# A three-stage spectral layer and a temporal layer on one core: the order of one hand-written period list

## The chip, the cores and the metric

The kernel runs on one core of one Trainium2 chip. The metric is the device time of one execution in microseconds (us). Three executions of the kernel before took 4318.21, 4323.12 and 4324.39 us; the median is 4323.12 us. Names of engines are those of the profile: PE (matmuls), PEld (loads of a matmul's weights), DVE, ACT, POOL (three engines for elementwise work), SP (a queue that only issues DMAs).

## The reference, cut to what matters

The input `x` is (4, 256, 256, 64) in float32: four images of 256 x 256 points with 64 channels. Two layers follow each other.

```python
h  = layernorm(x) @ w_te + b_te                        # 64 -> 128
F  = fft2(h)                                           # over both image axes
fc = gelu(concat(real(F), imag(F)) @ w_fc + b_fc)      # 256 -> 256, at every frequency
sp = real(ifft2(re(fc) + 1j * im(fc)))
x1 = x + sp @ w_tp + b_tp
d  = gelu(depthwise_conv3x3(layernorm(x1) @ w_fe + b_fe))
x2 = x1 + d @ w_fp + b_fp                              # end of layer 0
...
trend = moving_average(x2, 25)                         # layer 1, along the first image axis
out   = trend + irfft(W * rfft(x2 - trend)[:128])      # W mixes frequencies, per channel
```

## The kernel before, in words

**Three streams.** Layer 0 is cut into three pipelines that run beside each other.

- The *forward* stream takes columns of `x`, two at a time, 32 chunks for each image. It loads a chunk (`fl`), computes layernorm (the ops below that begin with f), folds it (`fa`, `fb`, `fh0`, `fh1`), transforms it along the height with matmuls (`y0`, `y1`), copies the result out of PSUM (`yt0`, `yt1`) and stores it to DRAM (`y_d`).
- The *spectral* stream takes pairs of frequencies from `y_d`: transform along the width (`x`, copied by `xs`), mix of channels for two halves (`m0`, `m1`; copied by `gc0`, `gc1`; added by `b0`, `b1`; GELU by `g0`, `g1`; folded by `p0`, `p1`), projection (`z`, copied by `zs`), a transpose (`w`, copied by `zt`), and the way back along the width (`u`, copied by `us`, combined by `uc`, `uf`, which also store to `u_d`).
- The *convolution* stream takes chunks of eight columns, 32 for each image: load from `u_d` (`ul`, `UL`) and from `x` (`xl`, `XL`), transform back along the height (`s`), residual (`r0`, `r1`), layernorm (the ops that begin with c), transposes (`t0`, `t1`, copied by `tt0`, `tt1`), sums for a fast convolution (`T0`, `T1`), products (`gm`, `gh`, `em`, `eh`), their evictions and sums (`gc_0`, `gc_1`, `ec0`, `ec1`, `cf0`, `cf1`, `sp0`, `sp1`), GELU (`a0`, `a1`), projection (`o0`, `o1`, copied by `fs0`, `fs1`), transposes back (`ft0`, `ft1`) and the residual with the store (`st0`, `st1`).

Layer 1 (`layer1`, L1494) follows when all of layer 0 is done.

**What sets the order.** A schedule of PE, DVE, ACT and POOL is recorded by hand: each of these engines runs its instructions in the order in which the Python code calls the ops, and waits on semaphores for the others. SP's queue is not in that schedule; its order is chosen by the tool that builds the program. The order of the ops is a list of words such as `g1:-3`, one list for each phase. `period(n)` (L1679) walks a list once: word `op:k` runs `op` for chunk `n + k` (for the ops of the spectral pairs, two of them for each n, for pair `2(n - 35) + k`). `do` (L1636) runs an op's predecessors first where they have not run yet (`FOLLOWS`, `EARLY`); what has run already is not run again. The list `FULL` (L1585) serves the periods n = 72 to 131, 60 of them, in which all three streams are alive. Lists `MIXED` and `CONV` serve the later periods.

**PSUM.** In this phase six PSUM banks are shared by all matmuls (`BANKS`, L27). `bank` (L158) hands out the bank that has been free longest, in the order of the recording; `free` (L182) returns a bank when its evicting op is recorded. So the order of the list also decides whose eviction a matmul waits for. If no bank is free, `make_room` (L168) pulls an eviction forward.

**Engines and lines of the ops that the prediction uses.** PE: `s` L1041, `t0` `t1` L1088, `w` L823, `z` L805, `m0` `m1` L750, `y0` `y1` L615, `x` L725, `u` L856, `gm` and `em` L1166, `gh` and `eh` L1180, `o0` `o1` L1283, `ft0` `ft1` L1308. ACT: `gc0` `gc1` L764, `g0` `g1` L775, `fq` and `cq` L279 (squares), `fR` and `cR` L288 and L289, `cA` L354, `cB` L364, `cC` L375, `cp` L395 and L396 (steps of the reciprocal root), `xs` L740, `zs` L813, `zt` L833, `us` L873, `yt0` `yt1` L633, `tt0` `tt1` L1098 to L1100, `gc_0` L1209, `gc_1` L1212, `ec0` `ec1` L1200, `a0` `a1` L1276, `fs0` `fs1` L1294. DVE: `b0` `b1` L770, `st0` `st1` L1322, `fm` `cm` L294, `fr` `cr` L283, `cM` L315 (seed of the root), `r0` L1054, `r1` L1062, `cf0` L1233 and L1234, `cf1` L1239 to L1245, `fa` L582, `fb` L602, `uc` L887 and L888, `uf` L907 and L920. POOL: `p0` `p1` L781, `fh0` `fh1` L609, `fx` and `cx` L410, `sp0` `sp1` L1218, `T0` `T1` L1124 to L1132, and the small products of the root, L355, L365, L376, L397.

**Buffers.** Most tiles of the spectral stream have two buffers; `zs`, `xb` (written by `fh0`, `fh1`), `yt`, `xn` (written by `cx`) and `sq` have one.

Of the kernel before, what the change touches and what calls it, by code (L numbers as in the profile page):

```python
# [136 lines left out]
def conv_seq_kernel(ctx: ExitStack, tc: tile.TileContext, a: dict, tables: bass.AP, out: bass.AP):  # L137
    nc = tc.nc
    x = a["x"]
# [11 lines left out]
        x="xs", m0="b0", m1="b1", z="zs", w="zt", u="uc", s="r1", t0="tt0", t1="tt1", gm="cf0",  # L151
        em="ec1", o0="fs0", o1="fs1", ft0="st0", ft1="st1", y0="yt0", y1="yt1",
# [1421 lines left out]
    def numbered(text):  # L1574

        return [(w.split(":")[0], int(w.split(":")[1]) if ":" in w else 0) for w in text.split()]

    follows = {}
    for line in FOLLOWS.replace("\n", "|").split("|"):
# [3 lines left out]


    FULL = numbered("""  # L1585
        g1:-3 uc:-3 em:-4 eh:-4 b0:-2 ec1:-4 cm:-1 gh:-4 m0:-1 gc_0:-4 ec0:-4 a0:-5 cf0:-4 p0:-3
        g0:-2 m1:-1 fr:-1 fh1:-3 p1:-3 z:-3 gc1:-1 gc0:-1 b1:-1 fq:-1 o0:-5 fs0:-5 o1:-5 cx:-2
        fs1:-5 fh0:-3 b0:-1 y0:-3 ft0:-5 g1:-2 sp0:-4 w:-4 st0:-5 zs:-3 p0:-2 fR:-1 fm:-1 cc:-1
        yt0:-3 ft1:-5 fC:-3 p1:-2 fp:-2 xl XL t1:-2 ul fM:-1 fA:-2 st1:-5 sp1:-4 tt1:-2 s cl t0:-2
        w:-3 gc_1:-4 tt0:-2 r0 r1 cM:-1 fx:-2 T0:-2 T1:-2 z:-2 m1 gc1 fB:-2 y1:-3 yt1:-3 uf:-3 zs:-2  # L1590
        cr UL:1 x:1 xs:1 g0:-1 u:-2 x:2 b1 us:-2 m0 zt:-4 xs:2 gc0 zt:-3 cf1:-4 fl a1:-4 cA:-1 Ta:-2
        cB:-1 cq gm:-3 fa:-2 fb:-2 cC:-1 cR cp:-1
    """)

    MIXED = numbered("""
# [204 lines left out]
```

## Time and profile before

| | value |
|---|---|
| median of three executions | 4323.12 us |
| profiled execution, its own time | 4325.4 us |
| its span, first to last instruction | 4323.6 us |
| PE busy over the span | 4158.0 us, 96% |
| DVE, POOL, ACT busy | 3453.4, 3163.4, 2961.5 us (80, 73, 68%) |
| mean granted clock of PE | 0.984 |
| one period of `FULL` in the steady part | 26.9 us |

The profiled execution is 1.8 us outside its span, and 2.3 us over the median. A line of the timeline has the start and the length in us, engine, source line, operation, the tile that it writes and those that it reads, the shape, how many instructions were merged into the line, and in brackets how long the engine stood idle before it and what ended that. Each matmul stands in the records twice. [...] What PE achieves is read from the distance between starts.

The times of `r0` (L1054), one for each convolution chunk, give the length of every period. In `FULL`, the periods from 984 to 1549 us, from 1580 to 1661 us and from 1869 to 2380 us are of 26.9 us with few exceptions. The first five periods, the change from the first to the second image (one gap of 68 us for two periods), the few periods behind it and the last three differ.

### The profile page before, as it was taken

How to read it: one execution, taken by the hardware profiler on the slowest of the kernel's cores; microseconds unless marked ns; L12 is line 12 of the kernel's file. 1: busy time of each engine (PE TensorE's matmuls, PEld its weight loads, DVE VectorE, ACT ScalarE, POOL GpSimd, SP SyncE). 2: the span in 40 equal slices, each digit the busy share in tenths (PEclk: the TensorE clock that was granted, in tenths of full speed). 3: DMA queues.
4: the chain of work that ended last, by engine and by line, in shares of the span. 5: the costliest groups of instructions: out<-in, count | busy, mean ns of one | idle time of the engine just before them, and what ended most of it. 6: DMA issues, size and time to landing. Idle time of an engine off the chain costs nothing.

```text
span 4323.6 us, 67389 instructions
## 1 busy us (share of the span) xinstructions
PE 4158.0 (96%) x22443; PEld 2315.2 (54%) x22443; DVE 3453.4 (80%) x5234; ACT 2961.5 (68%) x5409; POOL 3163.4 (73%) x3156
## 2 busy tenths in 40 slices
PE   8999999899999999899999999999998899999999
PEld 4544444345555555455555566666665566654444
DVE  6968999779999998899999878888887799962222
ACT  3338998678888887788888777888885466641111
POOL 6869999688888887788888877888887588840000
PEclk9999999989999999999999999999999999999999
DMA  6664555535454544444444443344433544439995
GB/s 190 211 190 142 161 161 162 152 98 137 137 137 137 137 137 124 122 122 138 138 138 129 113 109 109 106 112 112 118 98 91 173 113 118 114 108 358 342 343 228
DMA packets 763906, 655.28 MB, mean 152 GB/s; under 512 B 46413, under 2 KB 657695, under 8 KB 755240
## 3 DMA queue, kind: packets, MB, share of 16 engines
q1 hardware_dynamic: 726696, 583.84, 46.5%
q10 hardware_dynamic: 36864, 67.13, 4.1%
q8 instruction: 180, 2.95, 0.3%
q14 instruction: 166, 1.36, 0.1%
HBM read 364.81 MB, written 286.00 MB: 151 GB/s over the span
## 4 chain that ended last, share of the span: by engine, by line
PE 42%; POOL 6%; DVE 4%; DMA 4%; ACT 3%; issue 1%; SPq 1%; ACTq 0%; POOLq 0%; DVEq 0%
PE ps_o L1504 9%; PE ps_h_c L1166 5%; PE ps_p L750 3%; PE ps_s_c L1041 3%; PE ps_h_c L1180 3%; PE ps_f_c L1283 3%; PE ps_hh_c L1166 2%; PE ps_z L805 2%; PE ps_t_c L1088 2%; PE ps_u L856 2%; PE ps_x L725 2%; PE ps_ft_c L1308 2%; DMA out_dram<-oc 1%; PE ps_zt L823 1%; POOL xb L609 1%
## 5 line engine op out<-in xcount | busy, mean ns | idle before, releaser
L770 DVE TENSOR_TENSOR g<-ps_p,g 128x512 f32<-128x512 f32 x1040 | 702.2, 683 | 127.9 <-ACT g L764 109.7
L781 POOL TENSOR_TENSOR g<-g 128x512 f32<-128x512 f32 (+1 forms) x520 | 677.9, 1315 | 98.5 <-ACT g L775 88.8
L775 ACT ACTIVATE g<-g,b_fc 128x1024 f32<-128x1024 f32 (+1 forms) x520 | 598.3, 1151 | 1.5 <-DVE g L770 1.4
L750 PE MATMUL ps_p<-xs,wp 64*128 64x512 f32 (+1 forms) x2080 | 561.1, 615 | 9.9 <-DVE g L770 2.7
L1166 PE MATMUL ps_h_c<-td,wc_main 128*128 128x256 f32 x2048 | 517.1, 391 | 7.3 <-DVE s_c L1234 0.8
L764 ACT COPY g<-ps_p 128x512 f32<-128x512 f32 (+1 forms) x520 | 298.0, 585 | 268.5 <-PE ps_p L750 101.1
L1504 PE MATMUL ps_o<-xc,mt 128*128 128x512 f32 x1024 | 443.3, 595 | 3.9 <-DVE oc L1518 3.8
L1166 PEld LDWEIGHTS ps_h_c<-td,wc_main 128*128 128x128 f32 x2048 | 370.1, 193 | 122.5 <-ACT zt L833 36.7
L1276 ACT ACTIVATE h_c<-h_c,b_conv 128x1024 f32<-128x1024 f32 x256 | 297.6, 1164 | 140.6 <-DVE h_c L1245 54.1
L1518 DVE TENSOR_SCALAR oc<-ps_o,b_fp 128x512 f32<-128x512 f32 x128 | 93.5, 749 | 351.4 <-DMA out_dram<-oc 196.7
L1516 ACT ACTIVATE oc<-ps_o,b_fp 128x512 f32<-128x512 f32 x128 | 86.2, 686 | 363.0 <-PE ps_o L1504 196.7
L1128 POOL TENSOR_TENSOR td<-tt 128x512 f32<-128x512 f32 x256 | 327.0, 1299 | 10.0
L1504 PEld LDWEIGHTS ps_o<-xc,mt 128*128 128x128 f32 x1024 | 195.3, 191 | 251.2 <-issue 236.0
L609 POOL TENSOR_TENSOR xb<-xt 128x512 f32<-128x512 f32 x224 | 285.4, 1282 | 54.5 <-DVE xt L602 41.1
L750 PEld LDWEIGHTS ps_p<-xs,wp 64*128 64x128 f32 x2080 | 189.3, 186 | 239.6 <-issue 84.7
L805 PE MATMUL ps_z<-g,w_tp 128*64 128x512 f32 x1024 | 288.7, 617 | 24.6 <-POOL g L781 19.9
L725 PEld LDWEIGHTS ps_x<-tab,yb 128*64 128x64 f32 x4064 | 235.0, 138 | 133.3 <-issue 69.2
L1322 DVE TENSOR_TENSOR st<-x_c,ps_ft_c 128x256 f32<-128x256 f32 x512 | 261.8, 602 | 44.4 <-PE ps_ft_c L1308 41.4
L615 PE MATMUL ps_y<-xb,tab 128*64 128x512 f32 x1024 | 273.4, 623 | 23.3 <-POOL xb L609 17.1
L1283 PE MATMUL ps_f_c<-h_c,w_fp 128*64 128x512 f32 x1024 | 266.3, 615 | 15.6 <-ACT h_c L1276 15.5
L1180 PE MATMUL ps_h_c<-td,wc_half 64*128 64x256 f32 (+1 forms) x2048 | 278.6, 396 | 2.4 <-POOL td L1132 1.1
L1041 PE MATMUL ps_s_c<-uc_c,tab 64*128 64x512 f32 x1024 | 259.6, 616 | 15.6 <-DVE uc_c L990 8.7
(201 smaller groups left out, 9559.4 us busy)
## 6 DMA issues: line engine op xcount, KB each, us to landing
y_d<-yt SPq DMA_DIRECT2D x256, 256.0 KB, 3.6
yb<-y_d SPq DMA_DIRECT2D x256, 256.0 KB, 4.0
u_d<-ut SPq DMA_DIRECT2D x256, 256.0 KB, 3.6
x_c<-in_x_dram SPq DMA_DIRECT2D x512, 128.0 KB, 3.6
x_d<-st SPq DMA_DIRECT2D x128, 512.0 KB, 5.1
xc<-x_d SPq DMA_DIRECT2D x64, 1024.0 KB, 8.5
out_dram<-oc ACTq DMA_DIRECT2D x256, 256.0 KB, 5.8
xt<-in_x_dram SPq DMA_DIRECT2D x504, 128.0 KB, 2.5
```

The lines of the kernel that those rows point to most:

```text
L609: engine.tensor_tensor(sums[j][:, i], x0, x1, (ALU.add, ALU.subtract)[i])
L750: nc.tensor.matmul(ps[:, :nf], wp[rows, cols], rhs[rows], start=True, stop=r == 1 or not pr["special"],)
L770: nc.vector.tensor_tensor(gt[:, i], re, gt[:, 1], op)
L775: nc.scalar.activation(g, g, AF.Gelu, bias=b_fc[:, half : half + 1])
L781: nc.gpsimd.tensor_tensor(g[:, 0], g[:, 0], g[:, 1], op)
L805: nc.tensor.matmul(ps[r * C : (r + 1) * C, :nf], w_tp, d[:, :nf], start=True, stop=True)
L1041: nc.tensor.matmul(pss[i], tb[i * C : (i + 1) * C], uc[i * C : (i + 1) * C, ::-1, 1 - r, :] if down else uc[i * C : (i + 1) * C, :, r, :], ...
L1128: tt_(new[:, k : k + 3 : 2], a_c, nb_e, op)
L1166: nc.tensor.matmul(product(j, k, par), wc_main[:, par, k, :], td[:, k, slots(j)].rearrange("p j q -> p (j q)"), start=k in (0, 1, 3), stop ...
L1180: nc.tensor.matmul(product(j, k, par)[:, dst.start * Q : dst.stop * Q], wc_half[lo : lo + C, k, :], td[lo : lo + C, k, src].rearrange("p j ...
L1283: nc.tensor.matmul(ps[par * C : (par + 1) * C], w_fp, gs[j][:, :, par, i0 : i0 + 2, :].rearrange("p r j q -> p r (j q)"), start=True, stop ...
L1504: nc.tensor.matmul(ps[:, :nf], mts[i // CM][:, i % CM, t, to * P : (to + 1) * P], xc[:, t, :, :, i, :], start=t == 0, stop=t == 1,)
```

## The change

Only the list `FULL` changes; no instruction is added or removed in any stream.

```diff
     FULL = numbered("""
-        g1:-3 uc:-3 em:-4 eh:-4 b0:-2 ec1:-4 cm:-1 gh:-4 m0:-1 gc_0:-4 ec0:-4 a0:-5 cf0:-4 p0:-3
-        g0:-2 m1:-1 fr:-1 fh1:-3 p1:-3 z:-3 gc1:-1 gc0:-1 b1:-1 fq:-1 o0:-5 fs0:-5 o1:-5 cx:-2
-        fs1:-5 fh0:-3 b0:-1 y0:-3 ft0:-5 g1:-2 sp0:-4 w:-4 st0:-5 zs:-3 p0:-2 fR:-1 fm:-1 cc:-1
-        yt0:-3 ft1:-5 fC:-3 p1:-2 fp:-2 xl XL t1:-2 ul fM:-1 fA:-2 st1:-5 sp1:-4 tt1:-2 s cl t0:-2
-        w:-3 gc_1:-4 tt0:-2 r0 r1 cM:-1 fx:-2 T0:-2 T1:-2 z:-2 m1 gc1 fB:-2 y1:-3 yt1:-3 uf:-3 zs:-2
-        cr UL:1 x:1 xs:1 g0:-1 u:-2 x:2 b1 us:-2 m0 zt:-4 xs:2 gc0 zt:-3 cf1:-4 fl a1:-4 cA:-1 Ta:-2
-        cB:-1 cq gm:-3 fa:-2 fb:-2 cC:-1 cR cp:-1
+        g1:-3 em:-4 b0:-2 ec1:-4 cm:-1 gh:-4 m0:-1 ec0:-4 fh1:-3 gc_0:-4 cf0:-4 a0:-5 g0:-2 m1:-1
+        p0:-3 fq:-1 p1:-3 z:-3 gc1:-1 fr:-1 gc0:-1 fs0:-5 o0:-5 o1:-5 b1:-1 fa:-3 fs1:-5 fh0:-3
+        b0:-1 y0:-3 ft0:-5 g1:-2 fR:-1 sp0:-4 cx:-2 w:-4 ft1:-5 st0:-5 zs:-3 p0:-2 fC:-3 yt0:-3
+        cc:-1 xl fm:-1 p1:-2 t1:-2 ul tt1:-2 sp1:-4 fp:-2 fM:-1 s cl fl t0:-2 w:-3 fA:-2 st1:-5
+        gc_1:-4 fx:-2 r0 XL tt0:-2 r1 cM:-1 uf:-3 zs:-2 gc1 T0:-2 T1:-2 m1 UL:1 fB:-2 y1:-3 cA:-1 cr
+        g0:-1 yt1:-3 u:-2 x:2 b1 zt:-4 us:-2 zt:-3 m0 xs:2 cf1:-4 z:-2 x:1 xs:1 gc0 a1:-4 Ta:-2
+        cB:-1 fb:-2 cq gm:-3 cC:-1 uc:-2 cR cp:-1 eh:-3
     """)
```

With the pulls of `do` and `make_room` resolved, a steady period (the same in every one) reads on each engine as follows. Indices are those of the list; ACT is written from the same point, `g1:-3`. In `FULL`, `fA`, `fB`, `fC` and `fp` do nothing, since the root of the forward stream is taken together with that of the convolution stream in `cA` to `cp`.

```
PE   before  em eh gh m0:-1 m1:-1 z:-3 o0 o1 y0 ft0 w:-4 ft1 t1 s t0 w:-3 z:-2 m1:0 y1 x:1 u x:2 m0:0 gm
PE   after   the same circle, with u ahead of x:1
DVE  both    uc b0:-2 cm cf0 fr b1:-1 b0:-1 st0 fm st1 r0 r1 cM uf cr b1:0 cf1 fa fb
ACT  before  g1:-3 ec0 ec1 gc_0 a0 g0:-2 gc1:-1 gc0:-1 fq fs0 fs1 g1:-2 zs:-3 fR yt0 tt1 gc_1 tt0
             gc1:0 yt1 zs:-2 xs:1 g0:-1 us zt:-4 xs:2 gc0:0 zt:-3 a1 cA Ta cB cq cC cR cp
ACT  after   g1:-3 ec0 ec1 gc_0 a0 g0:-2 fq gc1:-1 gc0:-1 fs0 fs1 g1:-2 fR zs:-3 yt0 tt1 gc_1 tt0
             zs:-2 gc1:0 cA g0:-1 yt1 zt:-4 us zt:-3 xs:1 xs:2 gc0:0 a1 Ta cB cq cC cR cp
POOL before  p0:-3 fh1 p1:-3 cx fh0 sp0 p0:-2 p1:-2 sp1 fx T0 T1 cA cB cC cp
POOL after   fh1 p0:-3 p1:-3 fh0 sp0 cx p0:-2 p1:-2 sp1 fx T0 T1 cA cB cC cp
```

The calls that issue DMAs on SP stand in the order `xl XL ul st1 cl yt1 uf UL x fl` before and `xl ul cl fl st1 XL uf UL yt1 x` after. In the built programs the queue of a steady period is nearly the same in both: `xt` (four loads), the store of `st`, part of the four loads of `x_c`, two stores to `u_d`, two to `y_d`, two loads of `yb`, the rest of `x_c`, `uc`; one or two loads of `x_c` change places with these.

The last eviction that a matmul's PSUM bank waits for changes with the list (an op that takes two banks has two). `ft0` and `w:-4` also exchange theirs (`b1:-1` and `fs0`); ops not named keep theirs:

| matmul | before: banks freed by | after: banks freed by |
|---|---|---|
| `o1` | `gc1:-1` | `gc1:-1` |
| `s` | `st0`, `zs:-3` | `st0`, `zs:-3` |
| `w:-3` | `st1` | `tt1` |
| `z:-2` | `tt1` | `st1` |
| `m1:0` | `tt0`, `r0` | `r0`, `tt0` |
| `y1` | `r1` | `r1` |
| `u` | `yt1`, `zs:-2` | `zs:-2`, `gc1:0` |
| `x:1` | `gc1:0` | `yt1` |
| `x:2` | `xs:1` | `zt:-4` |
| `m0:0` | `b1:0`, `us` | `b1:0`, `us` |
| `gm` | `zt:-4`, `xs:2` | `zt:-3`, `xs:1` |
| `em` | `gc0:0`, `zt:-3` | `xs:2`, `gc0:0` |

(`em` is named here by the evictions of the period that it follows.)

## The prediction

> **What bounds the kernel now.** I read the page first, then the busy time by stretches, then the timeline of one steady period of `FULL` engine by engine, then the waits.
>
> ```profile
> span 4323.6 us, 67389 instructions
> PE 4158.0 (96%) x22443; PEld 2315.2 (54%) x22443; DVE 3453.4 (80%) x5234; ACT 2961.5 (68%) x5409; POOL 3163.4 (73%) x3156
> ```
>
> PE is busy 96% of the span. The list `FULL` rules 60 of the periods, some 1650 us. Two steady stretches of 18 periods each:
>
> ```profile
> 1065.00:1549.40 484.40, 480.48 (x2879) 265.76 (x2877) 451.47 (x670) 409.73 (x787) 426.64 (x397) 1.00 0.50 138
> 1868.90:2353.10 484.20, 480.77 (x2882) 265.55 (x2881) 451.64 (x667) 409.02 (x787) 427.28 (x397) 1.00 0.49 137
> ```
>
> Columns: stretch, length, busy time of PE, PEld, DVE, ACT, POOL, PE's clock, DMA share, GB/s. 484.4 / 18 = 26.9 us for a period. By busy time PE has no more than 0.2 us of it left, which would be 10 us in all. But a busy PE can hide a wait, so I compare starts of equal work:
>
> ```profile
> 1226.35 0.38 PE L1088 MATMUL ps_t_c<-ident,xn_c 128*128 128x128 f32 x2
> 1226.88 0.63 PE L823 MATMUL ps_zt<-ident,zs 128*128 128x128 f32 x4
> ...
> 1235.07 2.34 PE L1166 MATMUL ps_h_c<-td,wc_main 128*128 128x256 f32 x8
> 1237.25 1.89 PE L1166 MATMUL ps_hh_c<-td,wc_main 128*128 128x256 f32 x8
> 1238.98 1.89 PE L1166 MATMUL ps_h_c<-td,wc_main 128*128 128x256 f32 x8
> ```
>
> Eight records of the same shape take 2.18 us to the next line at 1235.07 (`gm`) and 1.73 at 1237.25. Record by record, starts are 0.216 apart when nothing is waited for; in `gm` three of the distances are 0.32, 0.46 and 0.32. The first 0.10 also stands in every change of row layout (1240.80, 1251.06) and stays; the other 0.35 is a wait. Likewise transposes follow each other in 0.109 us, but `w:-3` comes 0.386 after the last transpose of `t0` (1226.50 to 1226.88), and its second is 0.03 late: 0.30 of wait. Who ended them:
>
> ```profile
> 1226.13 0.61 DVE L1322 TENSOR_TENSOR st<-x_c,ps_ft_c 128x256 f32<-128x256 f32 x1
> ...
> 1249.85 1.08 DVE L1322 TENSOR_TENSOR st<-x_c,ps_ft_c 128x256 f32<-128x256 f32 x2
> 1251.39 1.25 DVE L294 TENSOR_REDUCE var_c<-sq 128x16 f32<-128x1056 f32 x1 [0.46 <-ACT sq L289]
> ```
>
> ```profile
> 1235.22 0.59 ACT L740 COPY xs<-ps_x 128x512 f32<-128x512 f32 x1 [0.88 <-PE ps_p L750]
> ```
>
> `st1` ends at 1226.74, 0.14 before `w:-3`, whose bank it frees. `xs:2` ends at 1235.81, 0.05 before the third record of `gm`, whose second bank it frees. `xs:2` itself starts only when `m0:0` has read the buffer that it overwrites, with ACT idle 0.88 us.
>
> [...]
>
> **The change part by part.** I walk one period, all times in the frame above (`z:-3` starts at 1245.31 before), lengths from the rows of the trace. From the end of an eviction to the matmul that waited for it I take 0.12 us (the rows show 0.12 to 0.14).
>
> *Banks of `gm`.* After, they come from `zt:-3` and `xs:1`, which ACT now runs ahead of `xs:2`, in the 0.88 us where it stood idle. `xs:1` ends about 1234.05, `gm` starts about 1234.8: minus 0.35 us. Its data, `T0`, ends 1234.2 (6.0 us of POOL from the end of `tt0`, 1228.14), 0.4 early enough.
>
> *Bank of `w:-3`.* After, it comes from `tt1`, which ends before 1253.1, with `w:-3` due at 1253.47: minus 0.30 us. `z:-2` takes over the bank of `st1`, 0.4 us later, free in time.
>
> *What holds `w:-3` otherwise.* `st1` was late as `fm` waited 0.46 us for `fR`. ACT now runs `fq` ahead of `gc1:-1`, in an idle 0.79 us, and `fR` ahead of `zs:-3`; `fm` follows `st0` at once, and DVE runs 0.46 us ahead from there. Cost if the cover is gone: `gc1:-1` waits for `z:-3` (1246.39 end, 1246.46 start before); `fq` occupies 0.97 us and would end at 1246.5 in the old frame. But `g1:-3` now ends before `eh`, so that `ec0` starts 0.18 earlier and `fq` is over at 1246.35. I take 0 here; at worst 0.2.
>
> *`fh0` ahead of `cx`.* `y0` waited for POOL, on average 0.19 us and more (1.86 to 2.20 us from `o0` to `y0`); now `fh0` ends 1.9 us earlier. Nearly no gain: the next bound is the chain `z:-3`, `gc1:-1`, `b1:-1`, `b0:-1`, `st0`, which frees the bank of `s`. It takes 1.15 + 0.59 + 2.8 + 1.08 + 0.12 = 5.74 us from the start of `z:-3` to `s`; PE takes 5.86 on average before. So minus 0.12. `cx` ends 2.95 us later (1.29 + 1.29 + 0.38), about 1248.7 with POOL's earlier start, `t1` is due at 1249.9: covered by 1.2 us; without that, each us is paid.
>
> *`cA` ahead of `g0:-1`.* It lets POOL begin the root when `T1` ends instead of standing 0.86 us; it needs the seed `cM`, ended 1229.56 before, wanted at 1229.9. ACT ends `g1:-3` some 0.8 us earlier.
>
> *`u` ahead of `x:1`.* No work changes. But `x:1` now takes the bank of `yt1`, which stands behind `cA` and `g0:-1` (1.05 us): it ends about 1231.7, `x:1` is due at 1231.8 to 1231.9. The cover is under 0.1 us; I charge 0.04, bounds 0 and 0.3. `x:2` takes that of `zt:-4`, 0.5 us early.
>
> *DMAs.* `fl`, `xl`, `ul`, `XL` and `yt1`'s store move on SP. `uc` was issued at 1237.11 for `s` at 1251.06, and takes 4 us; `xt` and `x_c` are a period ahead. I cost them at nothing; uncovered they would cost 3.6 us each to land, but their slack is ten. At the change of image (`XL` behind `r0`, `UL` ahead of `y1`) about 1 us may be lost or won, once.
>
> *Sum.* The circle of PE after: 26.9 - 0.35 (`gm`) - 0.17 (`w:-3`, as its average distance from `t0` is 0.665, against 0.494 without wait) - 0.12 (`s`) - 0.02 (`hh`) = 26.24. Charged 0.04 each for `x:1` and for `s`, both met with next to no slack: 26.32, so 0.58 us a period. PE is then at its own rate; DVE's 25.5 us (26.9 less its two idle stretches, 0.94 before `b1:-1` and 0.46 before `fm`) still fit. 43 periods are steady in the list of `r0`; with three of the others that look alike I take 46: 46 x 0.58 = 26.7 us. The 14 others, `MIXED`, `CONV` and layer 1 are costed at nothing. The profiled execution, 4325.4 (a span of 4323.6 and 1.8 around it), would become 4298.7; it lies 2.3 over the median of the three runs, so the median becomes 4296.4.
>
> **Rivals.**
>
> *Half of it or nothing.* `gc1:-1` behind `fq` comes 0.3 to 0.5 us late, `b1:-1` to `st0` and `s` with it, or `x:1` pays its 0.3. For: DVE's chain is the next bound with no slack. Against: the 0.18 us worked out above. It leaves 0.08 to 0.28 us of 0.58: 4310 to 4319, say 4315.
>
> *Slower.* ACT in order, with `cA` ahead of `g0:-1`, `yt1`, `zt:-4`, `us`: if DVE's seed comes late, all of these stand, and with them the banks of `x:1`, `x:2` and `m0:0`. `cM` stands behind `st1`, `r0` and `r1`, which wait for `s`. It decides when the seed ends more than 0.35 us (slack) + 0.1 (`x:1`) + 0.66 (all that is won) = 1.1 us later than before; from there each us costs 46. At 1.6 us late: 4323.1 + 46 x 0.5 = 4346. Against: DVE runs earlier, not later.
>
> *The change doesn't do what it says.* Several words (`fa:-3`, `fC:-3`, `em:-4`) resolve to the old place; if the bank waits reappear elsewhere at the same size, 4323.
>
> **How the numbers follow.** A measurement of this kernel can tell about 0.2% (8.6 us) from no change. Forecast 66% (4280 to 4309; 4280 is 60 periods at 0.66 and some us for the changes of stage), half or nothing 19%, slower 15%. Faster by over 0.2% (below 4314.5): 0.66 + 0.08 = 0.74; within: 0.11; slower: 0.15. The range leaves out 0.05 below and 0.13 above: 4280 to 4330.
>
> **What would show it.** Right: steady distances of `r0` near 26.3; `gm` 1.83 us to `hh`; `t0` to `w:-3` 0.49 us; no wait of `fm` for `fR`; `xs:2` still after `m0:0` with less idle. Wrong: `s` later than 5.74 us after `z:-3`; a wait of `x:1` behind `yt1`; ACT idle before `cA`; other lengths of the periods of `MIXED`.

## The result, and the profile after

The changed kernel takes 4288.74 us (median of four executions, 4282.18 to 4292.19), the kernel before 4320.84 (four executions, 4318.21 to 4324.39). The ratio is 0.9924, 95% interval 0.9911 to 0.9938: about 0.76% faster, 32 us. The forecast was 4296.4, in the range of 4280 to 4330. The number came out, but two errors of opposite sign stand behind it. The experiments are about the first of them, the steady periods.

The profiled execution of the changed kernel took 4282.18 us. Its first lines, and two steady stretches of 18 periods each (columns as in the prediction):

```profile
span 4280.0 us, 67389 instructions
PE 4123.3 (96%) x22443; PEld 2329.5 (54%) x22443; DVE 3453.5 (81%) x5234; ACT 2962.3 (69%) x5409; POOL 3174.2 (74%) x3156
```

```profile
1053.60:1531.00 477.40, 475.18 (x2881) 273.58 (x2882) 451.79 (x669) 410.61 (x788) 431.91 (x397) 1.00 0.51 140
1835.70:2313.30 477.60, 474.99 (x2881) 273.74 (x2882) 451.98 (x666) 410.22 (x787) 432.38 (x397) 1.00 0.50 138
```

477.5 / 18 = 26.5 us for a period, against 26.9. So a steady period wins 0.39 us and not the 0.58 of the forecast. The starts of `r0` tell where the profiled pair parts (before minus after):

| stretch | before, us | after, us | won |
|---|---|---|---|
| first six periods of `FULL` | 157.8 | 147.5 | 10.3 |
| next 25 periods | 676.3 | 665.3 | 11.0 |
| change of image (two periods) | 68.3 | 60.0 | 8.3 |
| five periods behind it | 140.0 | 136.3 | 3.7 |
| next 18 periods | 484.2 | 477.6 | 6.6 |
| last four of `FULL`; `MIXED` and `CONV` | 1457.2 | 1456.8 | 0.4 |

The steady stretches give 17.6 us, where 26.7 were forecast; start, change of image and the five periods behind it give 22 in this pair, where none were. These two executions differ by 43 us and the medians by 32: the one before lies 4.6 over its median, the one after 6.6 under. Some 3 us of the 43 lie behind the last `r0`, where no list differs. By the medians, 32 less 17.6, the other stages are worth some 14 us and not 22.

What the prediction looked for in the steady period is there, and one thing more. PE in the changed kernel, read by its starts, since a record of `gm` is 0.38 us long and the next begins 0.22 us behind it:

```profile
1221.25 1.99 PE L1166 MATMUL ps_h_c<-td,wc_main 128*128 128x256 f32 x8
1223.37 1.99 PE L1166 MATMUL ps_hh_c<-td,wc_main 128*128 128x256 f32 x8
1225.20 1.89 PE L1166 MATMUL ps_h_c<-td,wc_main 128*128 128x256 f32 x8
...
1239.08 0.66 PE L1088 MATMUL ps_t_c<-ident,xn_c 128*128 128x128 f32 x4
1239.57 0.60 PE L823 MATMUL ps_zt<-ident,zs 128*128 128x128 f32 x4
```

`w:-3` follows `t0` in 0.49 us, as without a wait, and the first line is shorter (1.99, before 2.34): `gm` has lost its wait. Yet the next line, below called `hh` (the second eight records of `gm`, which write the tile `ps_hh`), begins 2.12 us after it and not 1.83. That tile has a single buffer, and its last reader is the end of `cf1` on DVE:

```profile
1222.64 0.68 DVE L1245 SCALAR_TENSOR_TENSOR h_c<-ps_hh_c,s_c 128x512 f32<-128x512 f32 x1
```

It ends at 1223.32, `hh` starts at 1223.37. So of the two waits removed, 0.39 us came back at `hh`: it starts 0.29 us late, and from it to `em` there are 1.83 us, where 1.73 are the shortest. The other thing is on POOL, in the reciprocal root. Before, then after:

```profile
1235.88 1.28 POOL L1132 TENSOR_TENSOR td<-tt 128x512 f32<-128x512 f32 x1
1238.02 0.40 POOL L355 TENSOR_TENSOR newton_c<-newton_c,var_c 128x32 f32<-128x32 f32 x1 [0.86 <-ACT newton_c L354]
1238.86 0.29 POOL L365 TENSOR_TENSOR rstd_c<-newton_c,seed_c 128x32 f32<-128x32 f32 x1 [0.44 <-ACT newton_c L364]
1239.92 0.26 POOL L376 TENSOR_TENSOR newton_c<-newton_c,var_c 128x32 f32<-128x32 f32 x1 [0.77 <-ACT newton_c L375]
1241.03 0.25 POOL L397 TENSOR_TENSOR rstd_c<-newton_c,rstd_c 128x32 f32<-128x32 f32 x1 [0.85 <-ACT newton_c L396]
```

```profile
1222.20 1.29 POOL L1132 TENSOR_TENSOR td<-tt 128x512 f32<-128x512 f32 x1
1223.46 0.70 POOL L355 TENSOR_TENSOR newton_c<-newton_c,var_c 128x32 f32<-128x32 f32 x1
1224.59 0.25 POOL L365 TENSOR_TENSOR rstd_c<-newton_c,seed_c 128x32 f32<-128x32 f32 x1 [0.43 <-ACT newton_c L364]
1225.65 0.49 POOL L376 TENSOR_TENSOR newton_c<-newton_c,var_c 128x32 f32<-128x32 f32 x1 [0.81 <-ACT newton_c L375]
1226.99 0.25 POOL L397 TENSOR_TENSOR rstd_c<-newton_c,rstd_c 128x32 f32<-128x32 f32 x1 [0.85 <-ACT newton_c L396]
```

The root is a chain that goes to and fro between POOL and ACT. In the changed kernel these three waits are POOL's only ones of over 0.15 us in a whole period; the first of before is gone, since ACT runs L354 at 1216.37, ahead of `g0:-1`, and no longer behind `xs:2` and `a1`. From the end of L1132 to the end of L397 the mean of a steady period is 4.12 us before and 3.75 after; the rest of POOL's period is 22.78 and 22.75. The 0.37 between 4.12 and 3.75 is nearly the whole 0.39.

### The profile page after: what moved, and what is told of

It reads as the page before. It is cut to its first block, busy times and chain, and to the rows that moved or that the text cites. A ratio compares the mean times of both kernels' runs of the same rounds, so it can differ in the third digit from the quotient of the medians.

```text
span 4280.0 us, 67389 instructions
## 1 busy us (share of the span) xinstructions
PE 4123.3 (96%) x22443; PEld 2329.5 (54%) x22443; DVE 3453.5 (81%) x5234; ACT 2962.3 (69%) x5409; POOL 3174.2 (74%) x3156
## 4 chain that ended last, share of the span: by engine, by line
PE 47%; DVE 8%; DMA 2%; POOL 2%; ACT 1%; issue 1%; SPq 0%; DVEq 0%; POOLq 0%; ACTq 0%
PE ps_o L1504 9%; PE ps_h_c L1166 5%; PE ps_p L750 4%; PE ps_h_c L1180 4%; PE ps_f_c L1283 4%; PE ps_s_c L1041 3%; PE ps_hh_c L1166 3%; PE ps_z L805 3%; PE ps_u L856 2%; PE ps_x L725 2%; PE ps_t_c L1088 2%; PE ps_ft_c L1308 2%; PE ps_hh_c L1180 2%; PE ps_zt L823 1%; PE ps_y L615 1%
## 5 line engine op out<-in xcount | busy, mean ns | idle before, releaser
L1166 PE MATMUL ps_h_c<-td,wc_main 128*128 128x256 f32 x2048 | 500.5, 387 | 3.7 <-DVE g L770 1.4
L615 PE MATMUL ps_y<-xb,tab 128*64 128x512 f32 x1024 | 270.6, 614 | 10.8 <-POOL xb L609 9.2
L1283 PE MATMUL ps_f_c<-h_c,w_fp 128*64 128x512 f32 x1024 | 266.1, 614 | 15.2 <-ACT h_c L1276 15.2
```

The source lines that it names most:

```text
L1166: nc.tensor.matmul(product(j, k, par), wc_main[:, par, k, :], td[:, k, slots(j)].rearrange("p j q -> p (j q)"), start=k in (0, 1, 3), stop ...
L1283: nc.tensor.matmul(ps[par * C : (par + 1) * C], w_fp, gs[j][:, :, par, i0 : i0 + 2, :].rearrange("p r j q -> p r (j q)"), start=True, stop ...
```

## First experiments: the bank of `gm`, `cf1`, POOL's order

My theory after the result: the bank waits were the bound before; now the chain through `cf1` and the single buffer of `ps_hh` is. The rival: what the bank waits cost simply adds up.

**The bank of `gm` alone, put into the kernel before.**

```diff
-        cr UL:1 x:1 xs:1 g0:-1 u:-2 x:2 b1 us:-2 m0 zt:-4 xs:2 gc0 zt:-3 cf1:-4 fl a1:-4 cA:-1 Ta:-2
+        cr UL:1 x:1 g0:-1 u:-2 zt:-4 x:2 b1 us:-2 zt:-3 m0 xs:1 xs:2 gc0 cf1:-4 fl a1:-4 cA:-1 Ta:-2
```

> The kernel before with ACT's order of xs and zt alone changed: xs:1 and both zt:-4, zt:-3 swap places, so that the banks of gm are freed by zt:-3 and xs:1 and no longer by xs:2; the list of the other engines stays as before, so w:-3 still waits for st1. My theory (the gm wait goes, but hh then waits for the end of cf1, which holds the only buffer of the pair tile): the steady period goes from 26.90 to about 26.78 us, some 0.12 won in each of about 45 periods, the run to about 4316 us, and the profile shows hh starting right at the end of L1245. Rival (what the bank waits cost simply adds up): the whole 0.35 is won, the period is 26.55, the run about 4306 us.

Measured: 4325.41 us, ratio 1.0009 (1.0000 to 1.0017). `gm` takes 1.83 us, so its wait is gone, and the period of the second image is still 26.90; in the first image periods of 27.4 and 26.8 alternate. `x:2`, whose bank `zt:-4` now frees, comes 1.99 us after `u` and not 1.75. Both theories failed: nothing of the 0.35 was won.

**The same taken out of the changed kernel.**

```diff
-        g0:-1 yt1:-3 u:-2 x:2 b1 zt:-4 us:-2 zt:-3 m0 xs:2 cf1:-4 z:-2 x:1 xs:1 gc0 a1:-4 Ta:-2
-        cB:-1 fb:-2 cq gm:-3 cC:-1 uc:-2 cR cp:-1 eh:-3
+        g0:-1 yt1:-3 u:-2 x:1 xs:1 x:2 b1 us:-2 m0 zt:-4 xs:2 gc0 zt:-3 cf1:-4 a1:-4 Ta:-2 cB:-1
+        fb:-2 cq gm:-3 cC:-1 uc:-2 cR cp:-1 eh:-3
```

> The changed kernel with ACT's order of xs and zt put back, so that the second bank of gm is freed by xs:2 again; all else as in the changed kernel. My theory (the circle through cf1 and the pair tile sets the steady period, and gm's wait lies beside it): gm waits 0.35 us again, the wait of hh shrinks by as much, the period stays at 26.52 and the run at about 4288 us. Rival (bank waits add up): the period is 26.87 and the run about 4303 us.

Measured: 4328.96 us, ratio 1.0018 (1.0010 to 1.0027), period 27.38: worse than either theory. The bank of `x:2` is now freed by `xs:1`, which can only follow `x:1`, the matmul just ahead of `x:2`; so `x:2` waits 0.91 us (the two take 2.75 us, in the changed kernel 1.85). So this is no clean test of `gm`. It showed something else: `xs:2` is late, L364 behind it too, and POOL's wait for L364 is 1.47 us in the mean, while the rest of POOL's period is 22.8 us as ever.

**`cr` behind `cf1`.**

```diff
-        gc_1:-4 fx:-2 r0 XL tt0:-2 r1 cM:-1 uf:-3 zs:-2 gc1 T0:-2 T1:-2 m1 UL:1 fB:-2 y1:-3 cA:-1 cr
-        g0:-1 yt1:-3 u:-2 x:2 b1 zt:-4 us:-2 zt:-3 m0 xs:2 cf1:-4 z:-2 x:1 xs:1 gc0 a1:-4 Ta:-2
+        gc_1:-4 fx:-2 r0 XL tt0:-2 r1 cM:-1 uf:-3 zs:-2 gc1 T0:-2 T1:-2 m1 UL:1 fB:-2 y1:-3 cA:-1
+        g0:-1 yt1:-3 u:-2 x:2 b1 zt:-4 us:-2 zt:-3 m0 xs:2 cf1:-4 z:-2 x:1 xs:1 gc0 cr a1:-4 Ta:-2
```

> The changed kernel with one step moved on VectorE: cr, 1.13 us long, stands behind cf1 instead of behind cA, so that cf1 ends 1.13 us sooner. My theory: hh no longer waits for L1245, the 0.39 us in front of it goes, the steady period is about 26.13 us and the run about 4271 us. Rival (hh's gap is not the pair tile's): period 26.52, run 4288 us; a second way to fail is that whoever reads cr's result gets it too late, which would show as a wait for the line of cr.

Measured: 4287.80 us, ratio 0.9922 (0.9907 to 0.9936), period 26.52. My theory fell here. PE of this kernel:

```profile
2061.11 1.99 PE L1166 MATMUL ps_h_c<-td,wc_main 128*128 128x256 f32 x8
2062.94 1.89 PE L1166 MATMUL ps_hh_c<-td,wc_main 128*128 128x256 f32 x8
...
2071.91 2.41 PE L1283 MATMUL ps_f_c<-h_c,w_fp 128*64 128x512 f32 x8
2074.15 1.03 PE L615 MATMUL ps_y<-xb,tab 128*64 128x512 f32 x4
```

`hh` comes 1.83 us after `gm`, its wait is gone. But from L1283 to L615 there are now 2.24 us, in the changed kernel 1.84: the same 0.40 us, now at `o1`, whose bank `gc1:-1` frees on ACT. A wait that moves along when it is taken away is not the cause; it is where PE meets the engine that holds it. ACT had worked without a pause from the last step of the root to that `gc1:-1`.

**POOL's order of before, in the changed kernel.**

```diff
-        g1:-3 em:-4 b0:-2 ec1:-4 cm:-1 gh:-4 m0:-1 ec0:-4 fh1:-3 gc_0:-4 cf0:-4 a0:-5 g0:-2 m1:-1
-        p0:-3 fq:-1 p1:-3 z:-3 gc1:-1 fr:-1 gc0:-1 fs0:-5 o0:-5 o1:-5 b1:-1 fa:-3 fs1:-5 fh0:-3
-        b0:-1 y0:-3 ft0:-5 g1:-2 fR:-1 sp0:-4 cx:-2 w:-4 ft1:-5 st0:-5 zs:-3 p0:-2 fC:-3 yt0:-3
+        g1:-3 em:-4 b0:-2 ec1:-4 cm:-1 gh:-4 m0:-1 ec0:-4 gc_0:-4 cf0:-4 a0:-5 g0:-2 m1:-1 p0:-3
+        fq:-1 fh1:-3 p1:-3 cx:-2 z:-3 gc1:-1 fr:-1 gc0:-1 fs0:-5 o0:-5 o1:-5 b1:-1 fa:-3 fs1:-5
+        fh0:-3 b0:-1 y0:-3 ft0:-5 g1:-2 fR:-1 sp0:-4 w:-4 ft1:-5 st0:-5 zs:-3 p0:-2 fC:-3 yt0:-3
```

> The changed kernel with GpSimd's order of before: fh1:-3 behind p0:-3 and cx:-2 behind p1:-3 again. My theory (the first periods and the change of image gained because GpSimd hands p and g to TensorE sooner there): the steady period stays 26.52, the first six periods take 8 to 10 us longer again, the run about 4296 us. Rival (the start gained from the order of the other engines): the first six periods stay at 147.5 us and the run at 4288 us.

Measured: 4288.07 us, ratio 0.9924 (0.9910 to 0.9939); period 26.52; the first six periods take 151.1 us, 3.6 more than in the changed kernel. By this one profile POOL's order carries a third of what the start won, not all of it; in the median nothing of it is seen.

## Second experiments: POOL's circle

New theory: in the steady part POOL hardly ever waits but in the root, so its work and the root's way to ACT and back make a circle, a chain of work and waits that comes back to its own start in the next period, and this circle sets the period. The step to test is `cA`, which the prediction had costed at nothing.

**`cA` early, in the kernel before.**

```diff
-        cr UL:1 x:1 xs:1 g0:-1 u:-2 x:2 b1 us:-2 m0 zt:-4 xs:2 gc0 zt:-3 cf1:-4 fl a1:-4 cA:-1 Ta:-2
+        cr UL:1 x:1 xs:1 cA:-1 g0:-1 u:-2 x:2 b1 us:-2 m0 zt:-4 xs:2 gc0 zt:-3 cf1:-4 fl a1:-4 Ta:-2
```

> The kernel before with one word moved: ScalarE's part of the root's first step, cA:-1, stands ahead of g0:-1 instead of behind a1:-4. New theory (GpSimd's own circle sets the steady period: it works without a pause except where it waits for ScalarE in the four steps of the root; cA early takes the first of these waits, 0.72 us, away): the period goes from 26.90 to about 26.5 us although no bank of TensorE's changes hands, the run to about 4306 us; if TensorE's two bank waits then bind, 26.6 and 4311. Rival (the bank waits are what counts): 26.90 and 4323.

Measured: 4315.95 us, ratio 0.9992 (0.9985 to 0.9999), period 26.86. POOL no longer waits for L354, but now for L364:

```profile
2063.14 0.71 POOL L355 TENSOR_TENSOR newton_c<-newton_c,var_c 128x32 f32<-128x32 f32 x1
2064.82 0.40 POOL L365 TENSOR_TENSOR rstd_c<-newton_c,seed_c 128x32 f32<-128x32 f32 x1 [0.98 <-ACT newton_c L364]
```

Something else holds the kernel before at 26.86, and here it is POOL that has time: its wait for L364 is 0.85 us in the mean, where the kernel before has 0.43. L364 stands on ACT behind `xs:2`, and ACT stood idle for 0.88 us until `m0:0`, on PE, let `xs:2` start.

**`cA` late, in the changed kernel.**

```diff
-        gc_1:-4 fx:-2 r0 XL tt0:-2 r1 cM:-1 uf:-3 zs:-2 gc1 T0:-2 T1:-2 m1 UL:1 fB:-2 y1:-3 cA:-1 cr
-        g0:-1 yt1:-3 u:-2 x:2 b1 zt:-4 us:-2 zt:-3 m0 xs:2 cf1:-4 z:-2 x:1 xs:1 gc0 a1:-4 Ta:-2
+        gc_1:-4 fx:-2 r0 XL tt0:-2 r1 cM:-1 uf:-3 zs:-2 gc1 T0:-2 T1:-2 m1 UL:1 fB:-2 y1:-3 cr g0:-1
+        yt1:-3 u:-2 x:2 b1 zt:-4 us:-2 zt:-3 m0 xs:2 cf1:-4 z:-2 x:1 xs:1 gc0 a1:-4 cA:-1 Ta:-2
```

> The changed kernel with cA:-1 put back behind a1:-4; all banks stay as in the changed kernel. GpSimd's circle: it waits for cA again, 0.7 us or so, the period is about 26.9 to 27.0 us and the run about 4306 to 4310. Rival (bank waits): 26.52 and 4288.

Measured: 4306.80 us, ratio 0.9966 (0.9953 to 0.9979), period 26.86. So all of the change but `cA`, with both bank waits gone, wins 0.04 us a period. POOL's wait for L354 is back, and PE shows it as a longer wait in front of `hh`:

```profile
2050.59 0.65 POOL L355 TENSOR_TENSOR newton_c<-newton_c,var_c 128x32 f32<-128x32 f32 x1 [0.61 <-ACT newton_c L354]
```

```profile
2049.86 2.00 PE L1166 MATMUL ps_hh_c<-td,wc_main 128*128 128x256 f32 x8 [0.47 <-DVE h_c L1245]
```

**The square `cq` out of the root, in the changed kernel.**

```diff
-        g0:-1 yt1:-3 u:-2 x:2 b1 zt:-4 us:-2 zt:-3 m0 xs:2 cf1:-4 z:-2 x:1 xs:1 gc0 a1:-4 Ta:-2
-        cB:-1 fb:-2 cq gm:-3 cC:-1 uc:-2 cR cp:-1 eh:-3
+        g0:-1 yt1:-3 u:-2 x:2 b1 zt:-4 us:-2 zt:-3 xs:1 cq m0 xs:2 cf1:-4 z:-2 x:1 gc0 a1:-4 Ta:-2
+        cB:-1 fb:-2 gm:-3 cC:-1 uc:-2 cR cp:-1 eh:-3
```

> The changed kernel with the square cq (1.05 us on ScalarE) moved out from between the second and the third step of the root, where GpSimd waits for it, into the idle 1.27 us ahead of xs:2. GpSimd's circle: its wait in front of L376 shrinks from 0.82 to about 0.45 us, the period goes from 26.52 to about 26.15, the run to about 4272. Rival (VectorE's circle through cf1 and the single pair tile sets the period): 26.52 and 4288, with hh waiting for L1245 as before.

Measured: 4273.26 us, ratio 0.9896 (0.9881 to 0.9910), period 26.18. POOL's wait in front of L376 fell from 0.82 to 0.34 us, where 0.45 was worked out; PE's banks are handed out as in the changed kernel:

```profile
2050.58 0.36 POOL L376 TENSOR_TENSOR newton_c<-newton_c,var_c 128x32 f32<-128x32 f32 x1 [0.34 <-ACT newton_c L375]
```

**`cr` behind `cf1` as well** (both edits above together).

> As the run before it, and cr behind cf1 as well, so that hh waits neither for GpSimd's circle nor for L1245. GpSimd's circle: about 26.1 us, at most 2 us of the run better than with cq alone, about 4270. Rival (VectorE's circle): 26.52 without cr moved, and lower only with it.

Measured: 4267.44 us, ratio 0.9883 (0.9868 to 0.9897), period 26.12. This is the best version here: the changed kernel has 0.9924, so the difference is 0.4%, some 18 us. `cr` behind `cf1`, worth nothing while POOL's circle was longer, now takes away the last 0.06 us in front of `hh`. PE is busy in every moment of the steady stretch, the distances between its starts in the table below are within 0.05 us of their shortest, and POOL now waits 0.12 us elsewhere than in the root:

```profile
1055.00:1530.00 475.00, 475.00 (x2906) 277.21 (x2906) 451.50 (x674) 414.10 (x795) 435.61 (x399) 1.00 0.51 141
```

So 26.12 us is, as near as these runs show it, PE's own rate.

## Third experiments: the other circle, in the kernel before

**`cA` early and `zt` ahead of `xs`.**

```diff
-        cr UL:1 x:1 xs:1 g0:-1 u:-2 x:2 b1 us:-2 m0 zt:-4 xs:2 gc0 zt:-3 cf1:-4 fl a1:-4 cA:-1 Ta:-2
+        cr UL:1 x:1 cA:-1 g0:-1 u:-2 zt:-4 x:2 b1 us:-2 zt:-3 m0 xs:1 xs:2 gc0 cf1:-4 fl a1:-4 Ta:-2
```

> The kernel before with the two edits together that did nothing singly: cA:-1 ahead of g0:-1, and ScalarE's zt:-4 and zt:-3 ahead of xs:1 and xs:2. GpSimd's circle: with cA alone GpSimd's wait only moved from L355 to L365 (0.86 us), since L364 stands on ScalarE behind xs:2, gc0, zt:-3 and a1; with zt:-3 out of this row L364 comes 0.49 us sooner, L365 waits 0.43, the period is about 26.45 to 26.5 us and the run about 4302 to 4305, though neither edit alone won anything. Rival (the effects of the two edits add): 26.86 and 4316.

Measured: 4323.75 us, ratio 1.0008 (0.9999 to 1.0016), period 26.92: missed. `x:2` waits 0.36 us for `zt:-4`, which stands behind `cA` and `g0:-1`; in the changed kernel `u` ahead of `x:1` hides this.

**`cA` early and `zt:-3` behind `cB`.**

```diff
-        cr UL:1 x:1 xs:1 g0:-1 u:-2 x:2 b1 us:-2 m0 zt:-4 xs:2 gc0 zt:-3 cf1:-4 fl a1:-4 cA:-1 Ta:-2
-        cB:-1 cq gm:-3 fa:-2 fb:-2 cC:-1 cR cp:-1
+        cr UL:1 x:1 xs:1 cA:-1 g0:-1 u:-2 x:2 b1 us:-2 m0 zt:-4 xs:2 gc0 cf1:-4 fl a1:-4 Ta:-2 cB:-1
+        zt:-3 cq gm:-3 fa:-2 fb:-2 cC:-1 cR cp:-1
```

> The kernel before with cA:-1 ahead of g0:-1 and zt:-3 moved the other way, behind cB on ScalarE; gm's bank is still freed by xs:2, so TensorE keeps its wait of 0.35 us there. GpSimd's circle: L364 comes as early as with zt:-3 ahead of xs:2, the period is about 26.5 us and the run about 4302 to 4306 with the bank wait in place. Rival (the bank of gm has to be freed for the gain): 26.86 and 4316.

Measured: 4320.71 us, ratio 0.9999 (0.9990 to 1.0007), period 26.87: missed too. POOL's wait for L364 fell to 0.48 us, that for L375 rose to 1.30, since `zt:-3` now stands between. What stays the same in the three kernels with `cA` early is PE's waits in `w:-3` and `s`; that in `gm` stays in two of them, and in the third the 0.36 us at `x:2` stand in its place.

**`fq` and `fR` late, in the changed kernel.**

```diff
-        p0:-3 fq:-1 p1:-3 z:-3 gc1:-1 fr:-1 gc0:-1 fs0:-5 o0:-5 o1:-5 b1:-1 fa:-3 fs1:-5 fh0:-3
-        b0:-1 y0:-3 ft0:-5 g1:-2 fR:-1 sp0:-4 cx:-2 w:-4 ft1:-5 st0:-5 zs:-3 p0:-2 fC:-3 yt0:-3
+        p0:-3 p1:-3 z:-3 gc1:-1 fr:-1 gc0:-1 fq:-1 fs0:-5 o0:-5 o1:-5 b1:-1 fa:-3 fs1:-5 fh0:-3
+        b0:-1 y0:-3 ft0:-5 g1:-2 sp0:-4 cx:-2 w:-4 ft1:-5 st0:-5 zs:-3 fR:-1 p0:-2 fC:-3 yt0:-3
```

> The changed kernel with fq and fR back at their places of before on ScalarE (fq behind gc0:-1, fR behind zs:-3). My prediction made this the step that frees VectorE of the 0.46 us of fm. GpSimd's circle: fm waits for fR again, the steady period stays at 26.52; the first periods and the change of image may lose a few us, the run is 4288 to 4295. Rival (the earlier fR carries part of the steady gain): 26.6 to 26.8 and 4292 to 4301.

Measured: 4288.69 us, ratio 0.9930 (0.9915 to 0.9944), period 26.50. `fm` waits 0.59 us for `fR` again, and the period does not follow: `w:-3` has its bank from `tt1` here and keeps its 0.49 us behind `t0`. `s` waits 0.11 us again, and `hh` as much less.

**`cA` early and `fq`, `fR` early, in the kernel before.**

```diff
-        g0:-2 m1:-1 fr:-1 fh1:-3 p1:-3 z:-3 gc1:-1 gc0:-1 b1:-1 fq:-1 o0:-5 fs0:-5 o1:-5 cx:-2
-        fs1:-5 fh0:-3 b0:-1 y0:-3 ft0:-5 g1:-2 sp0:-4 w:-4 st0:-5 zs:-3 p0:-2 fR:-1 fm:-1 cc:-1
+        g0:-2 m1:-1 fr:-1 fh1:-3 p1:-3 fq:-1 z:-3 gc1:-1 gc0:-1 b1:-1 o0:-5 fs0:-5 o1:-5 cx:-2
+        fs1:-5 fh0:-3 b0:-1 y0:-3 ft0:-5 g1:-2 sp0:-4 w:-4 fR:-1 st0:-5 zs:-3 p0:-2 fm:-1 cc:-1
...
-        cr UL:1 x:1 xs:1 g0:-1 u:-2 x:2 b1 us:-2 m0 zt:-4 xs:2 gc0 zt:-3 cf1:-4 fl a1:-4 cA:-1 Ta:-2
+        cr UL:1 x:1 xs:1 cA:-1 g0:-1 u:-2 x:2 b1 us:-2 m0 zt:-4 xs:2 gc0 zt:-3 cf1:-4 fl a1:-4 Ta:-2
```

> The kernel before with cA:-1 ahead of g0:-1, and fq ahead of gc1:-1, fR ahead of zs:-3 on ScalarE; gm's bank is still freed by xs:2. Two circles of nearly the same length before: TensorE's own (26.13 us of work and row changes, 0.35 of wait in gm, 0.32 in w:-3, 0.11 in s, sum 26.91) and GpSimd's with the late cA (26.86, as the run with cA late in the changed kernel shows). cA early shortens the second, fR early the first by 0.32, so the period falls to about 26.5 to 26.6 us and the run to 4304 to 4309, while cA alone gave 26.86. Rival (GpSimd's circle alone decides, and with cA early something other than TensorE's waits holds it at 26.86): 26.86 and 4316.

Measured: 4298.90 us, ratio 0.9951 (0.9935 to 0.9968), period 26.56. Three words moved give all but 0.05 us of a period's gain, and PE still has its bank wait in `gm`:

```profile
2048.18 2.34 PE L1166 MATMUL ps_h_c<-td,wc_main 128*128 128x256 f32 x8
2050.36 1.99 PE L1166 MATMUL ps_hh_c<-td,wc_main 128*128 128x256 f32 x8
...
2066.06 0.66 PE L1088 MATMUL ps_t_c<-ident,xn_c 128*128 128x128 f32 x4
2066.55 0.60 PE L823 MATMUL ps_zt<-ident,zs 128*128 128x128 f32 x4
```

The table has the distances on PE from the first start of a group to that of the next, means of 15 steady periods in us, at the places where the kernels differ most, and POOL's stretch from the end of L1132 to the end of L397:

| kernel | `s` to `t0` | `t0` to `w:-3` | `o` to `y0` | `gm` to `hh` | `hh` to `em` | root on POOL | period |
|---|---|---|---|---|---|---|---|
| before | 1.92 | 0.68 | 2.05 | 2.18 | 1.75 | 4.12 | 26.90 |
| before, `cA` early | 2.03 | 0.80 | 1.79 | 2.18 | 1.73 | 4.00 | 26.86 |
| before, `cA`, `fq`, `fR` early | 1.92 | 0.49 | 1.85 | 2.18 | 1.76 | 3.81 | 26.56 |
| after, `cA` late | 1.92 | 0.49 | 1.83 | 2.47 | 1.83 | 4.11 | 26.86 |
| after | 1.92 | 0.49 | 1.84 | 2.12 | 1.83 | 3.75 | 26.51 |
| after, `cq` and `cr` moved | 1.92 | 0.49 | 1.83 | 1.83 | 1.73 | 3.15 | 26.12 |

So the kernel before had two circles of the same length. One is PE's own, with waits for answers to its own earlier work: over 26.12 it has 0.11 in `s`, 0.31 in `w:-3` and 0.35 in `gm` (second row); with small differences elsewhere these make 26.86. The other is POOL's, with the late `cA`, 26.86 too (fourth row). Shorten one, and the other stays: 0.04 us either way. Shorten both, and 0.3 to 0.4 us is won. For PE's circle alone the kernel with `cA` late stands here, which has the other moves of the change too; `fq` and `fR` early without `cA` were not run.

## Why the prediction was right, and where it was wrong

**PE's waits as the bound: half of it.** The waits were rightly read, and `w:-3` and `s` belong to PE's circle: taking them out beside `cA` moved the period from 26.86 to 26.56. But only one of two circles was seen. That PE was busy in 99% of the steady stretch made me look for the answer in PE alone.

**"Banks of `gm`": minus 0.35 us.** This is the term that failed. The wait went, and its worth was next to nothing: from `gm` to `em` there are 3.93 us before and 3.95 after. (The 0.10 us that was set aside for a change of row layout is measured at the places named: 0.32 us to the next pair of records for 0.22 otherwise, and 0.53 for 0.43. It is not the same at every change: in the transposes at 1226.08 it is 0.06, 0.165 for 0.109.) The kernel with `cA`, `fq` and `fR` early keeps the wait and needs 26.56, the changed kernel has shed it and needs 26.51. That holds while POOL's circle stands at 26.5; what the wait would cost at 26.12 was not run. The sum took PE's waits as gains and asked what is late next only along PE's and DVE's chains (5.74 us from `z:-3` to `s`; where `s` waits, 5.61 are measured, and another 0.11 inside `s`). It never closed POOL's circle.

**"`cA` ahead of `g0:-1`": costed at nothing.** I wrote that it lets POOL begin the root at once instead of standing 0.86 us, and gave that no price. It is the step without which the steady gain is 0.04 us and not 0.39. POOL is busy for 427 of 484 us in the stretches that the prediction shows, and that looks like slack; but 2.8 of its 3.2 us of idle time in a period lie in the root, where they are a way to ACT and back and not time to spare.

**`w:-3`, `fR`, `gc1:-1` behind `fq`, `x:1`, `fh0` ahead of `cx`.** The distance of 0.49 us came as said; `fm` no longer waits for `fR`; `z:-3` to `s` is 5.63 us, before 5.86, so 0.23 came where 0.12 was worked out; `x:1` does not wait, and `gc1:-1` starts 1.2 us after `z:-3`, as before. "Less idle" ahead of `xs:2` was wrong: ACT stands 1.27 us there, having come earlier, and still waits for `m0:0`.

**The other stages: costed at nothing, worth nearly half.** The forecast had 26.7 us in the steady stretches, where 17.6 came, 9 too much; it had 0 in the other stages, where some 14 came by the medians (22 in the profiled pair). That the number was met is luck: these two errors all but cancel. The run with `cA` late shows the second part nearly by itself: steady gain 0.04 us a period, under 2 us in all, yet 12 us less than the kernel before on the same chip. In these stretches the clock takes part. Before, then after, the first six periods and the change of image:

```profile
826.50:984.30 157.80, 139.02 (x736) 69.99 (x736) 122.87 (x168) 110.82 (x212) 110.54 (x100) 0.90 0.31 88
1660.60:1728.90 68.30, 58.69 (x319) 32.03 (x318) 52.69 (x76) 45.28 (x87) 49.88 (x45) 0.93 0.46 126
```

```profile
826.60:974.10 147.50, 129.10 (x733) 67.27 (x734) 123.41 (x169) 110.32 (x212) 110.48 (x100) 0.95 0.34 96
1639.40:1699.40 60.00, 53.83 (x321) 30.68 (x322) 52.13 (x75) 44.77 (x87) 51.79 (x46) 1.00 0.51 138
```

In the first six periods PE's time without work is nearly the same, 157.80 - 139.02 = 18.8 us and 147.50 - 129.10 = 18.4; its busy time for the same matmuls is 9.9 us shorter, at a mean clock of 0.95 and not 0.90. The stretches at a clock of 0.50 are 826.5 to 828.6, 849.1 to 855.9, 862.8 to 873.0, 890.1 to 900.3 and 924.2 to 927.6 before, 32.7 us in all, with PE busy for 28.1, and 857.2 to 864.0 and 881.1 to 887.9 after, 13.6 us with PE busy for 8.3; the rest is at 1.00. My estimate: if work at 0.50 takes about twice the time of work at 1.00, as the eight records of `s` in the last section do (3.79 and 1.99 us), half of 28.1 less half of 8.3, 9.9 us, is the clock's: all of the difference. At the change of image the busy time is 4.9 us shorter and the idle time 3.4. One place of the start, before and after:

```profile
863.68 1.97 PE L805 MATMUL ps_z<-g,w_tp 128*64 128x512 f32 x2 [3.90 <-POOL g L781]
866.13 1.97 PE L805 MATMUL ps_z<-g,w_tp 128*64 128x512 f32 x2 [0.48 <-POOL g L781]
869.21 1.97 PE L615 MATMUL ps_y<-xb,tab 128*64 128x512 f32 x4 [1.11 <-POOL xb L609]
```

```profile
859.15 3.19 PE L805 MATMUL ps_z<-g,w_tp 128*64 128x512 f32 x4 [4.54 <-POOL g L781]
```

In this place PE waits three times for POOL before and once after, with `fh1` ahead of `p0` and `fh0` ahead of `cx`; with POOL's order put back in the changed kernel the three are there again (3.31, 0.48 and 1.11 us), and the six periods take 3.6 us longer. Before, a stretch at a clock of 0.50 begins in the wait of 3.90 us and lasts 10.2 us, from 862.8; after, one begins in the wait of 4.54 us and lasts 6.8, from 857.2. But one begins in a wait of 2.43 us too, as the last section shows, so what starts such a stretch was not shown; and the clock's part here is read from the windows, not shown by an experiment. No single part carries the start: against 147.5 us it takes 151.1 with POOL's order of before, 150.5 with `fq` and `fR` late, 149.1 with `cA` late, one profile each. Which part carries the change of image stays open: these three take 60.1, 60.8 and 62.3 us there, against 60.0 after and 68.3 before. It is not `cA`, `fq` and `fR`: put into the kernel before, these three words leave it at 66.1 (and the start at 153.4). The four other kernels made from the one before, which won at most 0.1% as a whole, take 154.9 to 155.7 us for the start and 65.5 to 66.8 for the change of image; so the profile before lies on the slow side at both places.

## What to carry to other kernels

An engine with idle time can still set the period: look at where its idle time lies, and if all of it is in one chain that goes to another engine and back, add its work and these waits, and compare the sum with the period. If taking a wait away only moves it to another place at the same size, it is where an engine meets the one that holds it, and the cause lies on the other side. Where two circles have the same length, single edits show nothing; test the pairs.

## What was not expected of the hardware

PE waited 2.43 us ahead of `s` at 822.73 us before and 2.42 at 824.57 after, for the same work. The eight records behind took 3.79 us before and 1.99 after. The windows have the clock, before and then after, in the third column from the end:

```profile
821.80:828.60 6.80, 5.87 (x16) 2.21 (x18) 2.81 (x5) 0.00 (x0) 0.00 (x0) 0.50 0.66 183
```

```profile
821.80:828.60 6.80, 4.21 (x29) 1.92 (x28) 4.01 (x7) 2.21 (x6) 1.27 (x1) 1.00 0.89 246
```

So a gap of the same length was followed by a clock of 0.50 in one execution and of 1.00 in the other, and its length alone did not decide. L355 on POOL took 0.40 and 0.54 us in two periods before (1238.02 and 2068.62), where it followed waits of 0.86 and 0.72 us, 0.65 after a wait of 0.61 with `cA` late in the changed kernel, and 0.70 us in the changed kernel (1223.46), where it followed another instruction at once. So the root's stretch won only 0.37 us when a mean wait of 0.71 us in front of it went.
